# A two-layer relational graph convolution: 46 of 196 octets of layer 2 read h from SBUF instead of gathering rows, and GpSimd clears a few bytes behind each gather

## The chip, the cores and the metric

The kernel runs on one core of one Trainium2 chip. The metric is device time in microseconds (us), the median of several runs. A core has five engines with queues of their own: TensorE (PE, with its weight loads shown as PEld), VectorE (DVE), ScalarE (ACT), GpSimd (POOL) and SyncE (SP). They run side by side and wait for one another through semaphores. Sixteen DMA engines move data between HBM and the on-chip memory SBUF; matrix products land in PSUM, eight banks.

## The reference

There are 12500 nodes with 128 float32 features, and 200000 edges with a source, a target and one of 8 relations. The edges are sorted by target. Two layers are computed, then a residual and a layer norm:

```
for l in range(2):
    W     = einsum('rb,bio->rio', comp[l], basis[l])      # 8 relation weights, 128 x 128
    msgs  = (h @ W[r] for all r)[src, et]                 # one row per edge
    mean  = segment_sum(msgs, dst * 8 + et) / max(count, 1)
    h     = relu(mean.sum over relations + h @ root[l] + bias[l]) + h
out = layernorm(x + h)
```

## The kernel before

**Tiles.** The edges are cut into 1563 tiles of 128, one edge per partition, and eight tiles make an octet; there are 196 octets (NQ). The nodes are cut into 98 blocks of 128 (NT). h is held transposed, features on partitions: `hT`, the first 98 x 128 columns of a large SBUF tile named `arena`. Before h is written there, the same space holds the edge lists and scratch of the preparation.

**Preparation.** From the sorted targets the kernel works out, for each edge, its relation and target slot (`kr`), one over the count of its segment (`w`), its target relative to a window of the output (`near`) and the row that it reads: `idx`, the source in layer 1, and `idy`, source x 8 + relation, in layer 2. A series of guards (`fails`, `check_all`) makes sure that the sorted, windowed path holds for this input; otherwise a slow general path runs instead.

**Layer 1** (`for o in range(NG - 3)`). For each octet GpSimd gathers 8 times 128 rows of x from HBM with an indirect DMA (`gather`, line 678), five octets ahead (AHEAD) into a ring of seven buffers (`rows_r`). VectorE builds, per tile, a one-hot matrix times `w` (`onehot`, line 1122). TensorE multiplies rows by one-hot (`means`, L1215), ScalarE copies the sums out of PSUM (`take_means`, `copy` at L628), TensorE applies the eight relation weights (`product`, L1247), and `place` (L1278) adds the result to the block of 128 targets it belongs to. When a block is complete, `finish` adds bias, relu and residual on VectorE and writes `hT`. From octet 50 (TABLE) on, `table` (L1346) multiplies each finished block by all eight weights of layer 2, and the result (8 rows per node) is stored to HBM as `y_d`. One or two of these table halves go into each octet, in the banks `pt_b` and `ct_b`.

**Layer 2** (`for q in range(NQ)`). Since the weights are already applied, an edge only needs its row of `y_d`: GpSimd gathers it (the same line 678, by `idy`). VectorE builds small one-hots of 32 columns per tile and one of 256 per octet (`slot_hots`, L1091 and L1094). TensorE sums the rows by slot (`slot_sums`, L1442, eight 128 x 32 matmuls in the bank `misc`), ScalarE copies the 128 x 128 sums (`ys`), and one octet later TensorE places them in the block (`place_sums`, L1467, with the root weight L1471 when a block opens). Finished blocks are turned back and normalised, eight at a time (`norm`, L1585 to L1613). The last four octets (from FULL on) take another way (`add_rows`). After each octet up to there, `keep_on` issues 12 (BURST) float16 matmuls 128 x 384 whose result nobody uses (L1483).

**Order.** Everything is issued by a planner (`Plan`): the Python code calls `vec`, `act`, `pe`, `pool` and `load` in the order in which each engine's queue shall run, with the cells that an operation reads and writes, and the planner puts semaphore waits before those that need them. Engines signal only at marked places (`plan.mark`). A gather waits for the buffer that it fills to be read, seven octets back, and for the octet four back on its DMA semaphore to have landed (`lanes`: "gq" has 4):

```
t, cell = rows_r.take()
...
plan.add("POOL", some(i0, i0 + n), reads,
         [cell + (0,), cell + (1,)] + (fix_rows_c if fixes else []), lane="gq",
         n=n + fixes, after=after)
```

Once layer 1 is over, its tiles are used again: `home(where, n, ...)` hands out parts of old tiles to layer 2's buffers.

## Time and profile before

| | us |
|---|---|
| median of 3 runs | 4645.08 |
| lowest and highest | 4639.48, 4657.33 |
| profiled execution, its own time | 4616.74 |
| its span, first to last instruction | 4614.8 |
| layer 1's gathers, 1563, busy | 1476.4 |
| layer 2's gathers, 1563, busy | 1475.0 |

Busy shares of the whole span: TensorE 53%, its weight loads 37%, VectorE 30%, ScalarE 10%, GpSimd 64%. The mean granted clock of TensorE is 0.723 of its full speed. The DMA engines moved 284.99 MB, 62 GB/s.

How to read the rows: a group names the line of the kernel, the engine, the operation, output<-input by the names of the tiles, and a count; then busy time in us and the mean of one in ns; then the idle time of the engine just before these instructions and what ended most of it. "issue" is idle time in which the engine waited for nothing that the profile shows; "remote" is a wait whose releaser the profile did not find. A timeline row has the start in us from the beginning, the length, the engine and the operation, and in brackets the idle time before it. Matmuls overlap in the pipeline, so the sum of their lengths is more than their busy time.

### The profile page before, as it was taken

How to read it: one execution, taken by the hardware profiler on the slowest of the kernel's cores; microseconds unless marked ns; L12 is line 12 of the kernel's file. 1: busy time of each engine (PE TensorE's matmuls, PEld its weight loads, DVE VectorE, ACT ScalarE, POOL GpSimd, SP SyncE). 2: the span in 40 equal slices, each digit the busy share in tenths (PEclk: the TensorE clock that was granted, in tenths of full speed). 3: DMA queues.
4: the chain of work that ended last, by engine and by line, in shares of the span. 5: the costliest groups of instructions: out<-in, count | busy, mean ns of one | idle time of the engine just before them, and what ended most of it. 6: DMA issues, size and time to landing. Idle time of an engine off the chain costs nothing.

```text
span 4614.8 us, 38428 instructions
## 1 busy us (share of the span) xinstructions
PE 2424.3 (53%) x14055; PEld 1713.5 (37%) x14055; DVE 1386.0 (30%) x4891; ACT 465.8 (10%) x1141; POOL 2953.5 (64%) x3135
## 2 busy tenths in 40 slices
PE   2666666555666566666644444444444444444445
PEld 1555554444555455555521222222222222222223
DVE  2544333333333233233312222222222222222223
ACT  0111112121211111111200000000000000000000
POOL 5666666666666666666556666666666666666664
PEclk9878777878777777777866666666666666666667
DMA  3111122223222222222221111112211212122121
GB/s 100 45 50 46 45 63 86 86 90 93 86 69 73 73 70 73 63 74 68 74 74 45 46 55 47 55 46 56 56 46 55 55 47 56 46 55 55 47 55 45
DMA packets 129830, 284.99 MB, mean 62 GB/s; under 512 B 54019, under 2 KB 61773, under 8 KB 129637
## 3 DMA queue, kind: packets, MB, share of 16 engines
q0 software_dynamic: 100064, 205.13, 17.1%
q10 hardware_dynamic: 16971, 52.05, 2.9%
q1 hardware_dynamic: 12602, 25.31, 1.6%
q8 instruction: 112, 1.84, 0.2%
q14 instruction: 81, 0.66, 0.0%
HBM read 223.63 MB, written 58.65 MB: 61 GB/s over the span
## 4 chain that ended last, share of the span: by engine, by line
another core or an unknown queue 41%; PE 32%; issue 20%; ACT 5%; DVE 2%; POOL 0%; DMA 0%; SPq 0%; ACTq 0%; POOLq 0%; DVEq 0%
PE y L1247 8%; PE y L1483 7%; PE s L1215 5%; PE po L1442 3%; ACT sT L628 2%; PE s L1467 2%; PE pt L1346 2%; PE po L1278 1%; ACT ys L628 1%; ACT y_row L628 1%; PE ct L1346 1%; DVE dm L1122 1%; PE po L1280 0%; PE s L1471 0%
## 5 line engine op out<-in xcount | busy, mean ns | idle before, releaser
L678 POOL DMA_INDIRECT rows<-in_x_dram,idx x1563 | 1476.4, 945 | 841.5 <-issue 438.7
L678 POOL DMA_INDIRECT rows<-y_d,idy x1563 | 1475.0, 944 | 768.9 <-issue 447.6
L1247 PE MATMUL y<-w_sb,sT 128*128 128x128 f32 x3136 | 544.9, 345 | 533.3 <-ACT ys L628 236.4
L1483 PE MATMUL y<-id_h 128*128 128x384 f16 x2304 | 598.3, 398 | 342.9 <-issue 335.2
L1247 PEld LDWEIGHTS y<-w_sb,sT 128*128 128x128 f32 x3136 | 512.0, 255 | 558.1 <-ACT ys L628 245.2
L1122 DVE TENSOR_SCALAR dm<-cols,kr,w 128x128 f32<-128x128 f16 x1563 | 526.1, 402 | 493.4 <-remote 232.4
L1091 DVE TENSOR_SCALAR sT<-cols,kr,w 128x32 f32<-128x32 f16 x1536 | 352.8, 302 | 724.7 <-remote 543.4
L1442 PE MATMUL po<-rows,sT 128*32 128x128 f32 x3072 | 173.5, 354 | 712.1 <-ACT ys L628 437.4
L1215 PEld LDWEIGHTS s<-dm,rows 128*128 128x128 f32 x3126 | 434.5, 217 | 175.3 <-ACT sT L628 106.3
L1483 PEld LDWEIGHTS y<-id_h 128*128 128x128 f16 x2304 | 259.7, 114 | 643.2 <-issue 563.8
L1215 PE MATMUL s<-dm,rows 128*128 128x128 f32 x3126 | 451.2, 303 | 81.3 <-ACT sT L628 61.7
L1442 PEld LDWEIGHTS po<-rows,sT 128*32 128x32 f32 x3072 | 102.2, 136 | 799.8 <-ACT ys L628 463.5
L628 ACT ACTIVATE sT<-s 128x512 f32<-128x512 f32 x391 | 212.4, 596 | 804.5 <-remote 543.6
L628 ACT ACTIVATE ys<-po 128x128 f32<-128x128 f32 x192 | 53.2, 277 | 2111.9 <-remote 1871.6
L1299 DVE TENSOR_TENSOR po<-po,carry 128x128 f32<-128x128 f32 x98 | 29.2, 298 | 663.1 <-remote 406.8
L1299 DVE TENSOR_TENSOR s<-s,carry 128x128 f32<-128x128 f32 x97 | 28.9, 298 | 616.4 <-remote 387.7
L1346 PE MATMUL pt<-w_sb,arena 128*128 128x512 f32 x258 | 156.3, 678 | 48.5 <-issue 41.2
L1467 PE MATMUL s<-pl,ys 128*128 128x256 f32 x288 | 139.6, 572 | 14.3 <-issue 14.2
L1278 PE MATMUL po<-pl,ys 128*128 128x256 f32 x392 | 138.9, 438 | 15.1 <-DVE pl L1130 6.5
L628 ACT ACTIVATE y_row<-pt 128x512 f32<-128x512 f32 x131 | 78.4, 598 | 659.2 <-remote 451.3
L1585 PE MATMUL po<-ident,wide 128*128 128x128 f32 x96 | 23.5, 388 | 193.6 <-ACT ys L628 153.3
L871 PE MATMUL ct<-arena,id_h 128*128 128x512 f16 (+1 forms) x188 | 75.5, 422 | 85.9 <-issue 44.5
(214 smaller groups left out, 1565.0 us busy)
## 6 DMA issues: line engine op xcount, KB each, us to landing
y_d<-y_row ACTq DMA_DIRECT2D x96, 512.0 KB
rows<-in_x_dram,idx POOLq DMA_INDIRECT x1563
rows<-y_d,idy POOLq DMA_INDIRECT x1563
x_g<-in_x_dram SPq DMA_DIRECT2D x24, 512.0 KB
out_dram<-x_g SPq DMA_DIRECT2D x12, 512.0 KB
arena<-in_L_gnn_basis_dram SPq DMA_DIRECT2D x2, 512.0 KB
w_d<-y_row SPq DMA_DIRECT2D x2, 512.0 KB
w_sb<-w_d SPq DMA_DIRECT2D x2, 512.0 KB
```

The source lines that it names most:

```text
L628: act(lambda: nc.scalar.activation(out_t, in_t, AF.Copy), reads, writes)
L678: ins.append(nc.gpsimd.indirect_dma_start(out=t[:, i - q * Q, :], out_offset=None, in_=table_t, in_offset=bass.IndirectOffsetOnAxis(ap=ids ...
L871: nc.tensor.matmul(ct[:, :nb, :], id_h, eq[:, s - s0, :nb, main], start=(s == 1), stop=False)
L1091: vec(in_turn([lambda i=i: nc.vector.tensor_scalar(t[:, i, :], cols[:, :2 * K], kr[:, i0 + i:i0 + i + 1], w[:, i0 + i:i0 + i + 1], op0=ALU ...
L1122: emits.append(lambda i=i: nc.vector.tensor_scalar(t[:, i - q * Q, :wide], cols[:, :wide], ids[:, i:i + 1], w[:, i:i + 1], op0=ALU.is_equa ...
L1215: last = nc.tensor.matmul(s_b[i // 4][0][:, i % 4, :], t[:, i, :], d[:, i, :], start=True, stop=True)
L1247: last = nc.tensor.matmul(y[:m], t[:, r, :nt, :].rearrange("p t k -> p (t k)"), w_sb[:, 0, r, :], start=(r == 0), stop=(r == R - 1))
L1278: ins = nc.tensor.matmul(a, o[:m], t[:m], start=opens, stop=last and not root_in)
L1346: pe(lambda: nc.tensor.matmul(hb[:n].rearrange("p r d -> p (r d)"), hT[:, j * P:j * P + n], w_sb[:, 1, k * H:(k + 1) * H, :].rearrange("p ...
L1442: last = nc.tensor.matmul(m0[i // 2 * 2 * K:(i // 2 + 1) * 2 * K, :], d[:, i, :], t[:, i, :], start=i % 2 == 0, stop=i % 2 == 1)
L1467: ins = nc.tensor.matmul(a, o[:m], t[:m], start=opens, stop=last and not root_in and not fixed)
L1483: last = nc.tensor.matmul(f[:, :3, :], id_h, rhs, start=True, stop=True)
```

## The change

Four things change.

1. **Routed octets.** Every fourth octet of layer 2 from 8 to 188, 46 in all (`ROUTED`), is no longer gathered. Its rows are picked on the chip from h. For that, `hT` is turned, block by block and in place, into rows (nodes on partitions) after the tables of a block are made: `turn_rows`, four blocks at a time, as further entries of the `tables` list in layer 1, and `turn_last` for the last six at the start of layer 2. `open_block` then turns a block back where layer 2 needs it transposed.
2. **Sorting in layer 1.** In layer 1, octets 96 to 142, the edges of one routed octet at a time are sorted into slots, for each half octet (BR = 2) 49 groups of 256 source nodes with 32 slots each (CAP): `groups_of` and `ranks_of` on VectorE, `earlier_of` and `slots_of` on TensorE, two ScalarE copies and three stores to HBM (`lo_d`, `sc_d`) on SP. `values` prepares the numbers for all 46 among the checks.
3. **Routing in layer 2.** The 46 x 7 steps (`route_step`) are spread over the octets, seven per four octets. A step compares the slots' node numbers with the partition number (`compare`, VectorE, two operations of 512 columns), picks rows of h by these one-hots (`pick_rows`, TensorE, 32 matmuls 128 x 32, and a ScalarE copy), makes one-hots of target and relation times the weight (`slots_in`, VectorE, four of 320 columns) and adds up (`add_up`, TensorE, four matmuls 320 wide). Once per octet the sums go through the eight relation weights (`relate`), and the result enters `place_sums` as a gathered octet's does. `slot_sums` moves to the bank `ct_b`. `keep_on` is removed.
4. **Clearing.** After every gather GpSimd clears 256 bytes per partition of a scratch tile in layer 1 and 128 in layer 2 (`pause`), and each clearing waits for the one before it.

Two guards are added to `fails`, one for the window of 40 target nodes and one for the 32 slots. The core of the diff:

```diff
-    BURST = 12
     DONE = NT - 4
     FULL = NQ - 4
+    BT = 4
+    CAP = 32
+    NW = 40
+    GU = P // CAP
+    NGH = -(-NT // 2)
+    NTL = -(-NGH // GU)
+    NGR = NTL * GU
+    TU = 4
+    SEG = R * NW
+    BR = 2
+    WHOLE = [[(b, v, GU) for v in range(u, u + TU)] for b in range(BR) for u in range(0, NTL - 1, TU)]
+    REST = [(b, NTL - 1, NGH - (NTL - 1) * GU) for b in range(BR)]
+    STEPS = WHOLE[:len(WHOLE) // 2] + [REST] + WHOLE[len(WHOLE) // 2:]
+    NU = len(STEPS)
+    EVERY = 4
+    TURN = 4
+    LATER = NT - 6
+    FROM = 1
+    ROUTED = list(range(FROM + 10 * EVERY // NU + 2, 192, EVERY))
+    NR = len(ROUTED)
+    SORT = 96
...
+    blank = keep([P, P // 2], F32, "blank").bitcast(mybir.dt.uint8)
+    paused, pauses = tc.alloc_semaphore("s_pause"), [0]
+
+    def pause(n):
+        if pauses[0]:
+            nc.gpsimd.wait_ge(paused, pauses[0])
+        nc.gpsimd.memset(blank[:, :n], 0).then_inc(paused, 1)
+        pauses[0] += 1
...
-        if q >= NQ:
+        if q >= NQ or l == 1 and q in ROUTED:
...
+                    pause((2 * P, P)[l])
...
+    def groups_of(j):
+        o, oc = oh_b[j % 2]
+        o3 = o.bitcast(F16).rearrange("p (t g) -> p t g", t=Q)
+        vec(lambda: nc.vector.tensor_tensor(
+            o3, cols[:, None, :NGR].to_broadcast([P, Q, NGR]), grp[:, j, :].unsqueeze(2).to_broadcast([P, Q, NGR]),
+            op=ALU.is_equal), ["cols", grp_b[1]], [oc])
+
+    def earlier_of(j):
+
+        o, oc = oh_b[j % 2]
+        o4 = o.bitcast(F16).rearrange("p (b t g) -> p b t g", b=2, t=BT)
+        b, bc = ct_b
+        c4 = b.rearrange("p t d -> p (t d)")[:, :Q * NGR].rearrange("p (b t g) -> p b t g", b=2, t=BT)
+
+        def emit():
+            last = nc.tensor.matmul(c4, tri, o4, start=True, stop=False)
+            for k in range(1, BT):
+                last = nc.tensor.matmul(c4[:, :, k:, :], every, o4[:, :, :BT - k, :], start=False, stop=k == BT - 1)
+            return last
+
+        pe(emit, [oc, tri_b[1], one_b[1]], [bc])
...
+    def ranks_of(j):
+        (o, oc), (vv, vc), (jt, jc), (ct, cc) = oh_b[j % 2], v_b[j % 2], j_b, count_b
+        b, bc = ct_b
+        o3 = o.bitcast(F16).rearrange("p (t g) -> p t g", t=Q)
+        c3 = ct.rearrange("p (t g) -> p t g", t=Q)
+        b3 = b.rearrange("p t d -> p (t d)")[:, :Q * NGR].rearrange("p (t g) -> p t g", t=Q)
+        j3 = jt.bitcast(F16).rearrange("p (t c) -> p t c", t=Q)
+        v4 = vv.bitcast(F16).rearrange("p (t v c) -> p t v c", t=Q, v=3)
+        vec(lambda: nc.vector.tensor_tensor(c3, b3, o3, op=ALU.mult), [bc, oc], [cc])
+        vec(lambda: nc.vector.tensor_reduce(rank[:, j, :], c3, axis=AX.X, op=ALU.add), [cc], [rank_b[1] + (j,)])
+        vec(lambda: nc.vector.tensor_tensor(
+            j3, cols[:, None, :CAP].to_broadcast([P, Q, CAP]), rank[:, j, :].unsqueeze(2).to_broadcast([P, Q, CAP]),
+            op=ALU.is_equal), ["cols", rank_b[1] + (j,)], [jc])
+        vec(lambda: nc.vector.tensor_tensor(
+            v4, j3[:, :, None, :].to_broadcast([P, Q, 3, CAP]), val[:, j].unsqueeze(3).to_broadcast([P, Q, 3, CAP]),
+            op=ALU.mult), [jc, val_b[1]], [vc])
...
+    def turn_rows(j0, b, bc):
+
+        j1 = min(j0 + TURN, NT)
+
+        def first_step():
+            def emit():
+                for j in range(j0, j1):
+                    n = rows_of(j)
+                    last = nc.tensor.transpose(b[:n, j - j0, :], hT[:, j * P:j * P + n], ident)
+                return last
+
+            pe(emit, [("h", j) for j in range(j0, j1)] + ["ident"], [bc])
+
+        def second_step(copy=copy):
+            parts = [(j0, j1)] if rows_of(j1 - 1) == P else [(j0, j1 - 1), (j1 - 1, j1)]
+            for a, c in parts:
+                n = rows_of(a)
+                copy(hT[:n, a * P:c * P].rearrange("p (j d) -> p j d", d=P), b[:n, a - j0:c - j0, :], [bc],
+                     [("h", j) for j in range(a, c)])
+            turned_back.update(range(j0, j1))
+
+        return first_step, second_step
...
+    def compare(t):
+
+        i, u = t // NU, t % NU
+        if i >= NR:
+            return
+        at_u = STEPS[u]
+        b0, v0, m = at_u[0]
+        (o, oc), (b, bc) = hot_b[t % 3], bits_b[i % 2]
+        b3 = b.bitcast(F16).rearrange("p (b n) -> p b n", b=BR)
+        if m == GU:
+            n, a = HC, b3[:, b0, v0 * P:v0 * P + HC]
+            outs = [o[:, c * HC:c * HC + n] for c in range(2)]
+        else:
+            n, a = m * CAP, b3[:, :, v0 * P:v0 * P + m * CAP]
+            outs = [o[:, c * HC:c * HC + BR * n].rearrange("p (b n) -> p b n", b=BR) for c in range(2)]
+        vec(in_turn([lambda c=c: nc.vector.tensor_scalar(outs[c], a, node_p[:, c:c + 1], None, op0=ALU.is_equal)
+                     for c in range(2)]), [bc, "node"], new(oc))
+        plan.mark("DVE")
...
+    def slots_in(t):
+
+        i, u = t // NU, t % NU
+        sg, sgc = segw_b[i % 2]
+        for b, v, m in STEPS[u]:
+            o, oc = slot_at(i, b, v)
+            n, x = m * CAP, b * NTL + v
+            vec(lambda o=o, n=n, x=x: nc.vector.tensor_scalar(
+                o[:n], segs[:n], sg[:n, x:x + 1], sg[:n, BR * NTL + x:BR * NTL + x + 1], op0=ALU.is_equal,
+                op1=ALU.mult), [segs_b[1], sgc], new(oc))
+        plan.mark("DVE")
...
+    def pick_rows(t):
+        i, u = t // NU, t % NU
+        (o, oc), (g, gc) = hot_b[t % 3], rows_b[t % 3]
+        b, bc = pt_b
+        at_u = STEPS[u]
+
+        def emit():
+            for x, (_, v, m) in enumerate(at_u):
+                for k in range(m):
+                    at = (x * m + k) * CAP
+                    for c in range(2):
+                        j = 2 * (v * GU + k) + c
+                        n = rows_of(j)
+                        last = nc.tensor.matmul(b[k * CAP:(k + 1) * CAP, x, :], o[:n, c * HC + at:c * HC + at + CAP],
+                                                hT[:n, j * P:(j + 1) * P], start=c == 0, stop=c == 1)
+            return last
+
+        js = sorted({2 * (v * GU + k) + c for _, v, m in at_u for k in range(m) for c in range(2)})
+        pe(emit, [oc] + [("h", j) for j in js], [bc])
+        plan.mark("PE")
+        n, m = len(at_u), at_u[0][2] * CAP
+        copy(g[:m, :n * P], b[:m, :n, :].rearrange("p t d -> p (t d)"), [bc], new(gc))
+        plan.mark("ACT")
...
+    def add_up(t):
+        i, u = t // NU, t % NU
+        g, gc = rows_b[t % 3]
+        at_u = STEPS[u]
+
+        def emit():
+            for x, (b, v, m) in enumerate(at_u):
+                o, n = slot_at(i, b, v)[0], m * CAP
+                z = order[b, v]
+                last = nc.tensor.matmul(seg_b[b][0].rearrange("p t d -> p (t d)")[:, :SEG], g[:n, x * P:(x + 1) * P],
+                                        o[:n], start=z in (0, NTL), stop=z in (NTL - 1, BR * NTL - 1))
+            return last
+
+        bs = sorted({b for b, _, _ in at_u})
+        pe(emit, [gc] + [slot_at(i, b, v)[1] for b, v, _ in at_u], [seg_b[b][1] for b in bs])
+        plan.mark("PE")
+        for k in range(BR):
+            if u == (NU // 2, NU - 1)[k]:
+                t_s, sc = sum_b[i % 2]
+                t4 = t_s.rearrange("p (r b n) -> p r b n", r=R, b=BR)
+                b, bc = seg_b[k]
+                copy(t4[:, :, k, :], b.rearrange("p t d -> p (t d)")[:, :SEG].rearrange("p (r n) -> p r n", r=R), [bc],
+                     new(sc + (k,)))
+                plan.mark("ACT")
...
+    def relate(i):
+        t_s, sc = sum_b[i % 2]
+        t4 = t_s.rearrange("p (r b n) -> p r b n", r=R, b=BR)
+        b, bc = misc
+        pe(in_turn([lambda r=r: nc.tensor.matmul(
+            b[:BR * NW, 0, :], t4[:, r].rearrange("p b n -> p (b n)"), w_sb[:, 1, r, :], start=r == 0, stop=r == R - 1)
+            for r in range(R)]), [sc + (k,) for k in range(BR)] + [("w", 1, r) for r in range(R)], [bc])
+        plan.mark("PE")
+        o, c = ys[ROUTED[i]] = ys_r.take()
+        copy(o[:BR * NW], b[:BR * NW, 0, :], [bc], [c])
+        plan.mark("ACT")
...
+    def route_step(t):
+
+        i, u = t // NU, t % NU
+        if u == 0 and i < NR:
+            unit_rows(i)
+        compare(t + 1)
+        if i < NR:
+            pick_rows(t)
+        if 0 <= t - 1 < NR * NU:
+            slots_in(t - 1)
+        if 0 <= t - 2 < NR * NU:
+            add_up(t - 2)
+        if u == 3 and i >= 1 and i - 1 < NR:
+            relate(i - 1)
+        if u == 1:
+            fetch_rows(i + 1)
+        if u == NU - 1:
+            fetch(i + 2)
...
-    def keep_on():
-        f = y_full[0]
-        rhs = id_h[:, None, :].to_broadcast([P, 3, P])
-
-        def emit():
-            for _ in range(BURST):
-                last = nc.tensor.matmul(f[:, :3, :], id_h, rhs, start=True, stop=True)
-            return last
-
-        pe(emit, ["id_h"], [y_full[1]])
...
+        if 0 <= o - SORT - 1 < NR:
+            ranks_of(o - SORT - 1)
+        if 0 <= o - SORT < NR:
+            groups_of(o - SORT)
+        plan.mark("DVE")
...
+                if i == 1 and SORT - 2 <= o < SORT + NR + 2:
+                    break
...
+        if q == 0:
+            turn_last()
+        if q == FROM - 1:
+            compare(0)
+        route(q, 0)
...
+        route(q, 1)
...
-            keep_on()
...
```

239 lines of the change are left out of this document (226 added, 13 removed).

## The prediction

> **What bounds the kernel now.** I read the page first, then the waits of GpSimd, then a table by stage, then the timeline of single engines. The page's span and its two groups of gathers (line, engine, operation, count, busy us, mean ns, idle before):
>
> ```profile
> span 4614.8 us, 38428 instructions
> ...
> L678 POOL DMA_INDIRECT rows<-in_x_dram,idx x1563 | 1476.4, 945 | 841.5 <-issue 438.7
> L678 POOL DMA_INDIRECT rows<-y_d,idy x1563 | 1475.0, 944 | 768.9 <-issue 447.6
> ```
>
> GpSimd's waits (us in total, times, longest):
>
> ```profile
> POOL rows L678 <- remote: 550.5, 200, 9.5
> POOL rows L678 <- PE s L1215: 118.1, 19, 30.9
> ```
>
> Three stages (from and to, length; busy us and count of PE, PEld, DVE, ACT, POOL; granted clock, DMA share, GB/s), the first in layer 1:
>
> ```profile
> 110.00:1200.00 1090.00, 683.63 (x3865) 566.85 (x3864) 416.19 (x1253) 184.15 (x396) 703.73 (x745) 0.79 0.24 69
> ...
> 2400.00:3000.00 600.00, 246.39 (x1542) 123.58 (x1546) 140.64 (x577) 20.70 (x78) 394.08 (x418) 0.64 0.18 50
> ...
> 3600.00:4560.00 960.00, 422.05 (x2730) 221.68 (x2731) 256.18 (x1053) 33.98 (x137) 624.90 (x662) 0.66 0.19 51
> ```
>
> GpSimd's gathers pace both layers. A gather is 0.944 us busy; with 0.30 us of issue it would recur every 1.25 us. But layer 1 takes 1090/745 = 1.46 us per gather, layer 2 takes 1560/1080 = 1.44. The rest, some 0.2 us, are the waits "remote" and "PE". The DMA engines are idle four fifths of the time, so no bandwidth holds them. What does is seen in the timeline, first VectorE's and GpSimd's at the start (start, length, engine, line):
>
> ```profile
> 48.06 0.67 DVE L861 TENSOR_TENSOR arena<-cols,arena 128x149 f16<-128x149 f16 x4 [18.97 <-remote]
> 70.46 0.67 DVE L861 TENSOR_TENSOR arena<-cols,arena 128x153 f16<-128x153 f16 x4 [21.73 <-remote]
> ...
> 86.27 0.70 DVE L861 TENSOR_TENSOR arena<-cols,arena 128x165 f16<-128x165 f16 x4 [0.34 <-PE ct L872]
> ```
>
> ```profile
> 75.32 0.94 POOL L678 DMA_INDIRECT rows<-in_x_dram,idx  x1 [0.30 <-issue]
> 107.16 0.94 POOL L678 DMA_INDIRECT rows<-in_x_dram,idx  x1 [30.90 <-PE s L1215]
> ```
>
> A ping-pong of VectorE and TensorE needs some 20 us a round while GpSimd gathers back to back (until 75.32), and under 1 us once it stands still (86.27). So gathers 1.25 us apart hold up the other engines' handovers. The same in layer 2, TensorE, ScalarE and GpSimd:
>
> ```profile
> 3472.67 0.67 PE L1442 MATMUL po<-rows,sT 128*32 128x128 f32 x16
> 3473.26 0.70 PE L1467 MATMUL s<-pl,ys 128*128 128x256 f32 x2
> 3473.80 2.11 PE L1483 MATMUL y<-id_h 128*128 128x384 f16 x12
> 3488.43 1.10 PE L1442 MATMUL po<-rows,sT 128*32 128x128 f32 x16 [12.52 <-issue]
> 3489.47 1.22 PE L1467 MATMUL s<-pl,ys 128*128 128x256 f32 x2
> 3490.48 0.64 PE L1471 MATMUL s<-id_r,w_sb 128*128 128x128 f32 x2
> ...
> 3497.24 0.48 PE L1483 MATMUL y<-id_h 128*128 128x384 f16 x1 [2.46 <-issue]
> ```
>
> ```profile
> 3488.10 0.28 ACT L628 ACTIVATE ys<-po 128x128 f32<-128x128 f32 x1 [18.85 <-remote]
> ```
>
> ```profile
> 3492.08 0.94 POOL L678 DMA_INDIRECT rows<-y_d,idy  x1 [0.30 <-issue]
> 3493.33 0.94 POOL L678 DMA_INDIRECT rows<-y_d,idy  x1 [0.31 <-issue]
> ...
> 3519.92 0.94 POOL L678 DMA_INDIRECT rows<-y_d,idy  x1 [0.30 <-issue]
> 3524.07 0.94 POOL L678 DMA_INDIRECT rows<-y_d,idy  x1 [3.21 <-remote]
> ```
>
> ScalarE copies at 3488.10 the sums that were multiplied at 3472.67. GpSimd meanwhile fills its seven row buffers and then stands 3.2 us (3519.92 to 3524.07). Sixteen gathers and one such stall are 16 x 1.25 + 2.9 = 22.9 us, 1.43 each. That every stage comes out near 1.4 suggests a limit there, from which a pitch of 1.25 only borrows.
>
> **The change, part by part.** The reckoning is against the profiled execution, 4616.7 us (its span 4614.8 and 1.9 around it); the median of the three runs shown, 4645.1, lies 28 us above it, which is added at the end.
>
> *Fewer gathers.* 46 x 8 = 368 gathers of layer 2 go: at 1.44 us that is 530 us of GpSimd, the most the routing can give. The unit to compare is a period of four octets, one of them routed: now 32 x 1.44 = 46.1 us.
>
> *The clearing.* Behind each gather stands a memset that waits for the memset before it, done over 1 us earlier; behind it queues the next gather. The nearest rows are GpSimd's first instructions:
>
> ```profile
> 1.52 0.12 POOL L764 IOTA part<- 128x1 int32 x1
> 1.60 0.34 POOL L765 IOTA iota_f<- 128x256 f32 x1
> 1.91 0.34 POOL L767 IOTA arena<- 128x224 int32 x1
> ```
>
> From start to start, one element takes 0.08 us and 256 take 0.31, by line 128 take 0.19. A fill of bytes may be quicker than an iota of words, so the lower end is 0.08 for both sizes; the upper is an iota's pitch plus another issue gap of 0.30, 0.5 and 0.6. I take 0.17 for 128 bytes and 0.22 for 256, near the iotas. What covers it: the waits of 550.5 + 118.1 us, 0.21 per gather, which the spacing must make needless. If they stay, it costs 1563 x 0.22 + 1195 x 0.17 = 550 us in full. Layer 1 then is 1.25 + 0.22 = 1.47 per gather against 1.46: nothing, with ends of -0.08 x 1563 = -125 (a short fill) and +0.35 x 1563 = +550 (a long one). The stand of 30.90 us at the start should shrink: I take -20.
>
> *Layer 1's new work.*
>
> ```profile
> L1593 DVE TENSOR_TENSOR x_g<-po,x_g 128x512 f32<-128x512 f32 x24 | 16.6, 692 | 241.5 <-PE po L1585 157.4 <-remote 84.2
> ```
>
> In octets 96 to 142 VectorE gets a one-hot of 416 elements and four operations of 256 to 768, by this row 3 us an octet: it is busy 416.19/1090 = 38%, 4.5 us of 11.7, and becomes 7.5. TensorE gets 12 short f16 matmuls an octet and 98 transposes in all, some 30 us; ScalarE 25 copies of 0.6 and two small ones an octet; SP three small stores an octet, ahead of x loads that nobody waits for. From octet 94 to 143 the tables lose their second place an octet and catch up after. All are hidden behind 11.7 us of gathers; without that cover the routing's part is 46 x 3 = 140 us. The last turns, the rank check and the first fetches at the border of the layers come where GpSimd waits for the table anyhow: +5.
>
> *TensorE in layer 2.* The 12 filler matmuls an octet go and the picks come. From start to start, eight matmuls 128x32 (3472.67) take 0.59 us in the quick stretch and 1.04 in the slow one (3488.43); a placing 256 wide 0.54 and 1.01. Picking is 24 such groups of eight and a small rest; 0.59 holds a drain and a wait, so back to back I take 0.45 (0.32 to 0.59): 11.2. Adding up is 26 matmuls 320 wide, at most 0.54 x 320/256 = 0.68 each, taken 0.58: 15.1. The eight relation weights 2; four placings 2.2; three slot sums 1.8; roots, transposes and norm 1.5. Sum 34 us a period; 38 by the upper ends; 61 at the slow stretch's prices. GpSimd needs 24 x 1.42 = 34.
>
> *VectorE in layer 2.* Today 256.18 us for 662/8 octets, 3.1 an octet. A routed one needs 12 compares of 512 elements (at most 0.69, taken 0.5) and 26 slots of 320 (0.27, the pitch in the row below, to 0.69; taken 0.45): 18, and 1.5 for the rest. A period: 3 x 3.1 + 19.5 = 29, at most 38. ScalarE needs 7. SP fetches 0.85 MB per routed octet, one octet ahead; with the DMA engines 19% busy this is covered.
>
> Here a rule speaks against the change. The row:
>
> ```profile
> 3492.26 2.16 DVE L1613 TENSOR_SCALAR x_g<-x_g,st 128x128 f32<-128x128 f32 x8
> ```
>
> These are eight operations from SBUF to SBUF as the new ones are, and the gathers at 3492.08 and 3493.33 beside them keep their 0.94 us and 1.25 us pitch. The Trainium skill, SBUF — State Buffer, section "SBUF: two separate sides", says that such VectorE operations can lock GpSimd out of a shared port for their whole length and so starve its descriptors. By that rule the 18 us of new work would come on top of GpSimd's 34. The trace does not agree with it here; it stays as rival C.
>
> *Sum.* GpSimd 34, TensorE 34, VectorE 29 a period: three engines so close, coupled by handovers, won't overlap fully, nor is the clock full throughout. I add 15% to 34: 39.5. Layer 2: 46 x (46.1 - 39.5) = -304. Start, border and layer 1: -15. 4616.7 - 304 - 15 = 4298; with the 28, 4326, say 4330.
>
> **The rivals.**
> *A, the forecast:* a period of 37 to 42, 4210 to 4445. For it: 34 us of work against 46 of gathers, and the routing leaves a whole step (some 5 us) between each maker and user.
> *B, slower: TensorE becomes the bound,* at a low clock or with handovers still held up. Layer 2's granted clock is 0.64 to 0.66, and at 3497.24 a matmul that waits for nothing is issued 2.46 us late. 34 us at a clock of 0.68 are 50 us: 46 x 4 = +184, 4815. It decides above 46 us a period. Against it: where work is dense (3472.67) the prices are the low ones. The Trainium skill, TensorE: Matmul & The Clock Gate, Part 1, says that the clock halves after some 3.4 us of idling and is whole after as long a busy time; by that B needs waits, not work.
> *C, the port:* 34 us of GpSimd and 18 of VectorE in turn, 52: 46 x 6 = +276, 4905. It needs gathers that grow beside VectorE, which the rows deny.
> *D, GpSimd alone still paces:* both fills fit under 1.40, TensorE keeps up: a period of 34, -557, and layer 1 -95 to -125: 3950 to 4100.
> *E, a long fill:* 256 bytes cost 0.35, layer 1 +0.13 x 1563 = +203, layer 2 as in A: 4530.
> That the guards send the kernel to its general path is as good as excluded: in the reference's own inputs a half octet spans at most 37 nodes of 40 and fills 22 slots of 32.
>
> **How the numbers follow.** Chances: A 0.52, D 0.17, E 0.11, B 0.16, C 0.04. Within 0.5%, about what a measurement can tell, lies only the edge between E and B: 0.04. Faster takes A, D and most of E, 0.78; slower B and C with the worst of E, less that edge, 0.18. The range leaves out most of D, B and C below and above: 4080 to 4690.
>
> **What will show it.** Right: layer 2 has 1195 gathers; GpSimd's stalls of 3 us become even gaps; 24 gathers take near 39.5 us; TensorE's granted clock in layer 2 rises above 0.8; waits like 18.85 (ScalarE) shrink to a few us; 30.90 is shorter. Wrong: a pitch in layer 1 outside 1.40 to 1.55; gathers longer than 0.944 beside VectorE's compares; TensorE busy throughout at a low clock.

## The result, and the profile after

The changed kernel takes 5170.66 us, median of 4 runs (5162.00 to 5175.56); the kernel before, on the same chip, 4649.89 (4639.48 to 4657.33). The ratio is 1.112, with a 95% interval of 1.1091 to 1.1148: 11% slower, where 7% faster was forecast. Chips differ here, so a ratio is always taken against the kernel before on the same chip, and the text says how long that one took there.

The page of the kernel after, span and the two groups of gathers; below it, GpSimd's waits and the longest ones of ScalarE and VectorE:

```profile
span 5160.1 us, 81490 instructions
...
L741 POOL DMA_INDIRECT rows<-y_d,idy x1195 | 1162.6, 973 | 1321.4 <-PE ct L1882 1129.9
L741 POOL DMA_INDIRECT rows<-in_x_dram,idx x1563 | 1502.7, 961 | 301.7 <-issue 259.0
```

```profile
ACT sT L683 <- remote: 1274.4, 164, 53.1
POOL rows L741 <- PE ct L1882: 1129.9, 131, 56.1
DVE arena L1743 <- remote: 564.1, 75, 8.2
```

Layer 2 has 1195 gathers instead of 1563, but GpSimd now stands 1129.9 us before them, waiting for TensorE (L1882 is `slot_sums`, which reads the row buffers). The stages, with the columns as before (length; busy us and count of PE, PEld, DVE, ACT, POOL; clock, DMA share, GB/s):

```profile
110.00:1200.00 1090.00, 684.42 (x3918) 577.77 (x3917) 435.51 (x1312) 184.84 (x395) 950.30 (x1486) 0.81 0.23 66
2400.00:3000.00 600.00, 441.91 (x5106) 309.11 (x5110) 240.78 (x788) 60.91 (x150) 337.66 (x550) 0.86 0.17 48
3600.00:4560.00 960.00, 748.87 (x8667) 526.13 (x8666) 415.19 (x1372) 99.66 (x252) 493.43 (x800) 0.88 0.17 49
```

POOL counts two instructions per gather now, the gather and its memset. Layer 1 does 1486/2 = 743 gathers in the stretch where the kernel before did 745: unchanged. Layer 2 does 800/2 = 400 in 960 us, 2.40 us each; a period of four octets has 24, so 57.6 us against 46.1 before. No engine is full: TensorE 78%, GpSimd 51%, VectorE 43%, ScalarE 10%. It is 2814 us from the first to the last gather of layer 2, 2268 before: these 546 us are the whole loss, for the spans differ by 5160.1 - 4614.8 = 545.3.

The pitch inside a run of gathers (timeline of GpSimd near the start, in layer 1, then in layer 2):

```profile
74.71 0.95 POOL L741 DMA_INDIRECT rows<-in_x_dram,idx  x1 [0.17 <-issue]
...
110.75 0.95 POOL L741 DMA_INDIRECT rows<-in_x_dram,idx  x1 [0.17 <-issue]
...
600.65 0.95 POOL L741 DMA_INDIRECT rows<-in_x_dram,idx  x1 [0.17 <-issue]
601.59 0.34 POOL L703 MEMSET blank<- 128x256 uint8 x1
602.09 0.95 POOL L741 DMA_INDIRECT rows<-in_x_dram,idx  x1 [0.17 <-issue]
...
2320.86 0.95 POOL L741 DMA_INDIRECT rows<-y_d,idy  x1 [3.38 <-DMA y_d<-y_row]
...
2322.19 0.95 POOL L741 DMA_INDIRECT rows<-y_d,idy  x1 [0.17 <-issue]
2323.14 0.22 POOL L703 MEMSET blank<- 128x128 uint8 x1
2323.53 0.95 POOL L741 DMA_INDIRECT rows<-y_d,idy  x1 [0.16 <-issue]
```

With 256 bytes it is 602.09 - 600.65 = 1.44 us, with 128 bytes 1.34 (the median over layer 2 is 1.335). Without clearing it was 1.25. So 256 bytes cost 0.19 us and 128 only 0.085: the memset takes 0.22 us, but the issue gap in front of the next gather shrinks from 0.30 to 0.17. What happens between the runs of gathers (timeline of PE, ACT and POOL):

```profile
3502.71 0.28 ACT L683 ACTIVATE ys<-ct 128x128 f32<-128x128 f32 x1
...
3506.51 1.22 PE L1774 MATMUL pt<-arena,dm 128*32 128x128 f32 x8 [0.23 <-issue]
...
3512.66 0.95 POOL L741 DMA_INDIRECT rows<-y_d,idy  x1 [0.17 <-issue]
3513.19 0.60 ACT L683 ACTIVATE idx<-pt 128x512 f32<-128x512 f32 x1 [10.20 <-remote]
3513.84 3.48 PE L1774 MATMUL pt<-arena,dm 128*32 128x128 f32 x64 [4.58 <-issue]
...
3524.75 0.66 PE L1882 MATMUL ct<-rows,sT 128*32 128x128 f32 x16
...
3525.51 0.28 ACT L683 ACTIVATE ys<-ct 128x128 f32<-128x128 f32 x1 [2.40 <-PE ct L1882]
3525.74 0.95 POOL L741 DMA_INDIRECT rows<-y_d,idy  x1 [11.91 <-PE ct L1882]
```

By the rows, TensorE has picked the rows of h at 3507.73 (3506.51 + 1.22); ScalarE copies them 5.5 us later, at 3513.19, in the middle of the last gather of the run. TensorE, which has stood for 4.58 us by then, goes on at 3513.84, when the gather has just ended. Now GpSimd stands 11.91 us, until TensorE has worked itself forward to `slot_sums` (3524.75), which frees the row buffers. Then the next eight gathers follow, and the others stand again. GpSimd and the rest of the core take turns instead of working side by side.

### The profile page after: what moved, and what is told of

Read it like the earlier page. It is cut to its first block, busy times and chain, and to the rows that moved or that the text cites. A ratio compares the mean times of both kernels' runs of the same rounds, so it can differ in the third digit from the quotient of the medians.

```text
span 5160.1 us, 81490 instructions
## 1 busy us (share of the span) xinstructions
PE 3621.2 (70%) x32975; PEld 2733.0 (53%) x32975; DVE 2162.5 (42%) x6759; ACT 712.4 (14%) x1673; POOL 3482.7 (67%) x5525
## 4 chain that ended last, share of the span: by engine, by line
PE 51%; another core or an unknown queue 27%; issue 13%; ACT 4%; DVE 3%; POOL 2%; DMA 0%; ACTq 0%; POOLq 0%; DVEq 0%
PE pt L1774 12%; PE y L1318 8%; PE y L1796 7%; PE po L1796 6%; PE s L1286 5%; ACT sT L683 2%; PE po L1820 2%; PE pt L1417 2%; PE po L1349 2%; PE ct L1882 1%; POOL rows L741 1%; PE s L1907 1%; PE ct L1417 1%; DVE dm L1193 1%
## 5 line engine op out<-in xcount | busy, mean ns | idle before, releaser
L741 POOL DMA_INDIRECT rows<-y_d,idy x1195 | 1162.6, 973 | 1321.4 <-PE ct L1882 1129.9
L1774 PE MATMUL pt<-arena,dm 128*32 128x128 f32 (+1 forms) x18032 | 959.5, 313 | 463.1 <-ACT sT L683 208.5
L1774 PEld LDWEIGHTS pt<-arena,dm 128*32 128x32 f32 (+1 forms) x18032 | 723.3, 123 | 668.4 <-issue 283.4
L703 POOL MEMSET blank<- 128x256 uint8 (+1 forms) x2758 | 821.7, 298 | 1.6
L1743 DVE TENSOR_SCALAR arena<-y_row,sel 128x320 f32<-128x320 f16 (+1 forms) x598 | 235.0, 447 | 578.9 <-remote 299.2
L1743 DVE TENSOR_SCALAR arena<-y_row,comp_sb 128x320 f32<-128x320 f16 (+1 forms) x598 | 234.9, 448 | 572.8 <-PE y L1796 288.6
L1796 PE MATMUL po<-arena,sT 128*128 128x320 f32 (+1 forms) x798 | 275.3, 480 | 16.2 <-issue 15.3
L1724 DVE TENSOR_SCALAR dm<-arena,pair 128x512 f32<-128x512 f16 (+1 forms) x644 | 263.3, 458 | 9.5 <-remote 6.1
L1796 PE MATMUL y<-arena,sT 128*128 128x320 f32 x798 | 257.6, 458 | 3.6 <-issue 1.9
L1796 PEld LDWEIGHTS po<-arena,sT 128*128 128x128 f32 (+1 forms) x798 | 156.9, 207 | 110.9 <-issue 68.5
```

What stands on the lines that cost most here:

```text
L703: nc.gpsimd.memset(blank[:, :n], 0).then_inc(paused, 1)
L741: ins.append(nc.gpsimd.indirect_dma_start(out=t[:, i - q * Q, :], out_offset=None, in_=table_t, in_offset=bass.IndirectOffsetOnAxis(ap=ids ...
L1724: vec(in_turn([lambda c=c: nc.vector.tensor_scalar(outs[c], a, node_p[:, c:c + 1], None, op0=ALU.is_equal) for c in range(2)]), [bc, "node ...
L1743: vec(lambda o=o, n=n, x=x: nc.vector.tensor_scalar(o[:n], segs[:n], sg[:n, x:x + 1], sg[:n, BR * NTL + x:BR * NTL + x + 1], op0=ALU.is_equal,
L1774: last = nc.tensor.matmul(b[k * CAP:(k + 1) * CAP, x, :], o[:n, c * HC + at:c * HC + at + CAP], hT[:n, j * P:(j + 1) * P], start=c == 0, s ...
L1796: last = nc.tensor.matmul(seg_b[b][0].rearrange("p t d -> p (t d)")[:, :SEG], g[:n, x * P:(x + 1) * P], o[:n], start=z in (0, NTL), stop=z ...
```

## The experiments

Three theories stood against each other. The spacing theory: gathers that follow one another too closely hold up the handovers between the other engines, and 1.33 us is too close. The work theory: the routing itself costs TensorE, VectorE or a shared port this much. The per-gather theory: each gather holds the others up by a fixed amount, however it is spaced.

The chips turned out to be of two kinds. On some the kernel before takes 4613 to 4653 us, on one 3928. The one of 3928 was met a single time, so what sets it apart is not known, nor whether it lasts. The table gives the results; pitch is the median from gather to gather in layer 2, layer 2 runs from its first gather to its last, and the period is that length over 49.

| run | layer 2 clears | kernel before, us | this, us | ratio, 95% interval | pitch | layer 2, us | period |
|---|---|---|---|---|---|---|---|
| e3 | nothing | 3928 | 3714.41 | 0.9457, 0.9441 to 0.9472 | 1.25 | 1730 | 35.3 |
| e1 | 256 B | 3928 | 4136.57 | 1.0533, 1.0516 to 1.0551 | 1.44 | 1838 | 37.5 |
| e5, routing alone | 128 B | 3928 | 4011.19 | 1.0212, 1.0192 to 1.0233 | | 1717 | 35.0 |
| e4, clearing alone | 128 B | 3928 | 4385.65 | 1.1166, 1.1147 to 1.1184 | 1.33 | 2101 | |
| e8 | nothing | 4617 | 5264.92 | 1.1411, 1.1389 to 1.1434 | 1.25 | 2894 | 59.1 |
| e6 | 128 B | 4614 | 5054.34 | 1.0951, 1.0932 to 1.0969 | 1.34 | 2739 | 55.9 |
| e7 | 128 B | 4617 | 5059.22 | 1.0957, 1.0934 to 1.0981 | 1.34 | 2752 | 56.2 |
| e9 | 256 B | 4617 | 4777.69 | 1.0352, 1.0333 to 1.0370 | 1.44 | 2474 | 50.5 |
| e16 | 320 B | 4653 | 4706.94 | 1.0125, 1.0097 to 1.0153 | 1.50 | 2359 | 48.1 |
| e17 | 320 B | 4650.5 | 4716.75 | 1.0145, 1.0125 to 1.0164 | 1.50 | 2367 | 48.3 |
| e18 | 384 B | 4650.5 | 4443.63 | 0.9554, 0.9527 to 0.9581 | 1.55 | 2099 | 42.8 |
| e15 | 384 B | 4614 | 4274.16 | 0.9267, 0.9249 to 0.9285 | 1.55 | 1976 | 40.3 |
| e11 | 512 B | 4613 | 4358.34 | 0.9443, 0.9422 to 0.9465 | 1.66 | 2056 | 42.0 |
| e12 | 768 B | 4613 | 4555.09 | 0.9871, 0.9851 to 0.9892 | 1.87 | 2249 | 45.9 |
| e14 | 4 x 832 B per octet | 4614 | 5142.45 | 1.1137, 1.1109 to 1.1165 | 1.25 | 2851 | 58.2 |
| e13, routing alone | 128 B | 4613 | 4046.71 | 0.8769, 0.8744 to 0.8793 | | 1739 | 35.5 |
| e10, clearing alone | 128 B | 4617 | 4545.78 | 0.9844, 0.9826 to 0.9861 | 1.34 | 2254 | |

### The parts one by one, where the kernel before takes 3928 us

**e1: 256 bytes in layer 2 too.**

```diff
-                    pause((2 * P, P)[l])
+                    pause(2 * P)
```

> The changed kernel, but 256 bytes cleared behind layer 2's gathers too. Theory H (gathers closer than about 1.40 us hold up the other engines' handovers; 1.334 us in layer 2 of the changed kernel is too close): the pitch becomes 1.44, the waits of 8 to 12 us in layer 2 go, a period of four octets falls from 57 to about 40 us, the time to 4300 to 4500. Theory W (the routing's own work and chain of handovers need 57 us a period whatever GpSimd does): the period stays at 55 to 58, the time at 5100 to 5200.

**e3: the routing without the clearing.**

```diff
-                    pause((2 * P, P)[l])
```

> The changed kernel without any clearing: gathers 1.25 us apart. H: layer 2 gets worse than the changed kernel's 57 us a period, 60 or more, and the stalls of 3 us are back in layer 1, whose length stays within 1%; 5250 or more. W: layer 2 as in the changed kernel, 5150 to 5200.

**e4: the clearing without the routing**, put into the kernel before.

```diff
                         in_offset=bass.IndirectOffsetOnAxis(ap=ids[:, i:i + 1], axis=0)))
+                    pause((2 * P, P)[l])
```

> The kernel before with the clearing alone (256 and 128 bytes), no routing, the filler matmuls kept. H: the clearing fills the time that stalls took, 4600 to 4700 in all. If instead the clearing adds to the stalls: 1563 x 0.19 + 1563 x 0.085 = +430, about 5080.

**e5: the routing with hardly a gather beside it**, one of eight in layer 2.

```diff
-            plan.add("POOL", some(i0, i0 + n), reads,
+            m = 1 if l == 1 and SOON // Q < q < NQ - 4 else n
+            plan.add("POOL", some(i0, i0 + m), reads,
```

> The changed kernel with one gather of eight in the octets 3 to 191 of layer 2 (seven of eight tiles sum rows that are old, so the result is not the reference's): TensorE, VectorE and ScalarE keep all their work. H: the period is TensorE's own work, 37 to 42 us, the time 4250 to 4450. W: 55 us or more, 5000 to 5200.

All four fell on a chip on which nothing is held up, and none of the four times lies where it was expected: the kernel before takes 3928 us there, and in e4, which has all its gathers, GpSimd has next to no stand. The groups of gathers on the page of e4, and layer 2's in e3:

```profile
L686 POOL DMA_INDIRECT rows<-in_x_dram,idx x1563 | 1487.9, 952 | 271.2 <-issue 265.9
L686 POOL DMA_INDIRECT rows<-y_d,idy x1563 | 1487.4, 952 | 269.1 <-issue 269.1
```

```profile
L741 POOL DMA_INDIRECT rows<-y_d,idy x1195 | 1268.8, 1062 | 461.2 <-issue 349.8
```

In e4 nearly all idle time is "issue", the 0.17 us before each instruction. There the clearing is a plain cost, 1563 x (0.19 + 0.085) = 430 us worked out and 4385.65 - 3928.07 = 458 measured, and the routing alone, e3, gains 5.4%. Layer 2 of e3 and of e5 (a stretch of 600 us each):

```profile
2700.00:3300.00 600.00, 595.06 (x8845) 443.74 (x8844) 421.57 (x1411) 106.92 (x258) 441.36 (x410) 1.00 0.27 79
```

```profile
2700.00:3300.00 600.00, 595.06 (x8891) 444.45 (x8894) 421.03 (x1418) 106.78 (x258) 67.62 (x102) 1.00 0.13 41
```

TensorE is busy 99% at a clock of 1.00 in both, with 410 gathers in the stretch or with some 50; the period is 35.3 and 35.0 us. So the routing's own work is 35 us of TensorE a period, nothing is lost to gathers beside it, and the work theory cannot account for 57. What this chip could not show is the holding up itself.

### The change again, and its parts, where the kernel before takes 4614 us

**e6 and e7: the changed kernel, unedited**, beside the kernel before.

> The changed kernel itself, beside the kernel before, where the kernel before gathers without stalls (3928 us, 1.257 us per gather). Theory S (the clearing is pure cost wherever the handovers aren't held up; the routing saves): layer 1 grows by 1563 x 0.19 = 300, layer 2 is TensorE's 36 us a period plus what the memsets add, together 4030 to 4110, 2 to 5% slower than the 3928. Theory F (the two kernels stand as in the recorded pair): 1.11 times the kernel before, 4370.

> The changed kernel once more, so that the three kernels beside it can be held against it on the same chip. Where the kernel before needs some 4600 us: 1.10 times that, as twice before. Where it needs some 3930: by the parts, layer 1 + 300 and layer 2 near TensorE's 36 us a period, 4030 to 4110.

**e8: e3's kernel. e9: e1's. e10: e4's.**

> The changed kernel without any clearing. Where the kernel before needs some 3930 us: again 3714. Where it needs some 4600 us: theory H says that gathers 1.25 us apart hold up handovers, that the routing has many more of them than the kernel before and so loses more than with the clearing: 5100 or more. Theory K (the clearing costs there as well, and the routing alone pays): below the kernel before, 4300 to 4500.

> The changed kernel with 256 bytes cleared in layer 2 too, 1.44 us per gather. Where the kernel before needs some 3930 us: again 4137. Where it needs some 4600 us: theory H says that 1.44 is wide enough, layer 2's period falls from 57 to 40 us, 4300 to 4500; if the handovers stay held up, above 4900.

> The kernel before with the clearing alone, no routing. Where the kernel before needs some 3930 us: again 4386. Where it needs some 4600 us: theory H says that the clearing takes the place of the stalls, 4500 to 4650; if it adds to them, 5000.

The loss is there again, 9.5%. Taking the clearing out makes it worse (e8, 1.141), more of it makes it better (e9, 1.035), though e9's 4778 us lie between its two expectations, 4300 to 4500 and above 4900. GpSimd's stands for TensorE in layer 2, in e8 and in e9:

```profile
POOL rows L741 <- PE ct L1881: 1347.0, 135, 56.1
```

```profile
POOL rows L741 <- PE ct L1882: 646.7, 87, 50.7
```

The clock of e9 rises with it, against 0.86 to 0.88 in the kernel after:

```profile
2700.00:3300.00 600.00, 513.90 (x6181) 365.67 (x6182) 312.06 (x991) 74.53 (x180) 385.07 (x567) 0.93 0.19 55
```

The kernel of e8 stands 103.4 us for this wait in e3, on the other chip:

```profile
POOL rows L741 <- PE ct L1881: 103.4, 21, 45.0
```

Routing, code and data are the same, and layer 2 takes 1730 us on the one chip and 2894 on the other. And e10 separates the parts from the other side: without the routing the clearing costs nothing on this chip but gains 1.6%, its 0.19 and 0.085 us a gather taking the place of stands, just as the prediction had it.

### More room behind each gather

**e11: 512 bytes in layer 2. e12: 768 bytes.** The scratch tile is too small for it, so `base`, free by then, is cleared.

```diff
-        nc.gpsimd.memset(blank[:, :n], 0).then_inc(paused, 1)
+        t = blank if n <= 2 * P else base.rearrange("p b a c -> p (b a c)").bitcast(mybir.dt.uint8)
+        nc.gpsimd.memset(t[:, :n], 0).then_inc(paused, 1)
...
-                    pause((2 * P, P)[l])
+                    pause((2 * P, 4 * P)[l])
```

> The changed kernel with 512 bytes cleared behind layer 2's gathers (by 0.107 us per 128 bytes a pitch of 1.66 us, 24 gathers 40 us). Where the kernel before needs some 4600 us: theory H, that only the spacing of the gathers is short, says the handovers come free, a period of 40 to 43 us, 4270 to 4420, faster than the kernel before; if every gather holds them up whatever the spacing (theory G), the time stays near the 4778 of 256 bytes or above. Where it needs some 3930: GpSimd paces layer 2, 2280 + 1990 = 4280.

> The same with 768 bytes, a pitch of 1.87 us, 24 gathers 45 us. H: GpSimd paces layer 2 evenly, 45 to 46 us a period, 4500 to 4560 on either kind of chip. G: above 4700 where the kernel before needs some 4600.

**e13: e5's kernel**, nearly without gathers.

> The changed kernel with one gather of eight in the octets 3 to 191 of layer 2 (seven of eight tiles sum old rows). H and G: with the gathers nearly gone nothing holds up the handovers, layer 2 runs at TensorE's own 35 us a period also where the kernel before needs some 4600 us: 4010 to 4060. If that chip has slow handovers for another reason than gathers: 4500 or more.

The stands are gone: in e11 all of GpSimd's idle time before layer 2's gathers but 2.5 us is issue. With its gathers a quarter further apart (1.66 for 1.34) the change takes 14% less time (0.9443 against 1.0951). The page of e11, and layer 2 of e11 and of e13:

```profile
L742 POOL DMA_INDIRECT rows<-y_d,idy x1195 | 1156.3, 968 | 196.4 <-issue 193.9
```

```profile
2700.00:3300.00 600.00, 546.65 (x7655) 404.31 (x7646) 472.18 (x1236) 91.73 (x222) 542.84 (x696) 0.97 0.23 66
```

```profile
2700.00:3300.00 600.00, 595.05 (x8830) 445.25 (x8829) 415.24 (x1397) 106.13 (x257) 68.53 (x100) 1.00 0.12 39
```

e13 has the same 595 us of 600 and the same clock as on the chip of 3928 us. That refutes the work theory for this chip as well, and e11 refutes the per-gather theory: it has all 1195 gathers, and no copy is held up for long (counted below). With 768 bytes GpSimd is full, and something else shows, which the last section takes up.

### The gap or the mean rate

**e14: the same mean rate as e11, but in bursts.** The eight gathers of an octet follow one another without clearing, and four memsets of 832 bytes stand behind them.

```diff
-                    pause((2 * P, P)[l])
+                    if l == 0:
+                        pause(2 * P)
+                for _ in range(4 * (l == 1 and i1 - i0 == Q)):
+                    pause(6 * P + 64)
```

> The changed kernel, with layer 2's clearing behind each gather taken out and four clearings of 832 bytes put behind every eight gathers instead. Gathers of an octet then follow one another at about 1.25 us, and the mean pitch stays near 1.65. If the mean rate decides (the chip's kernel before near 4615): no handover is held up, layer 2 as with 512 bytes, some 2060 us, the whole about 4360. If the gap behind each gather decides: TensorE and ScalarE stand for most of each burst of 8 x 1.25 = 10 us and catch up in the pause of about 3 us; an octet then takes 13 to 16 us, layer 2 2150 to 2500, the whole 4450 to 4800. On a chip whose kernel before takes near 3930 nothing is held up in either case, and GpSimd paces at about 1.65: layer 1 2290, layer 2 2030 to 2060, the whole about 4350.

**e15: 384 bytes**, e11's edit with `3 * P`.

> The changed kernel with 384 bytes cleared behind each gather of layer 2: a pitch of about 1.55, between 1.44 (256 bytes) and 1.66 (512). If handovers come free at a point below 1.55: GpSimd paces, 1.55 x 1195 and a little more, layer 2 1900 to 1950 us, the whole 4200 to 4260, faster than with 512 bytes. If they come free step by step: layer 2 between the 2474 and 2056 us of its neighbours, about 2200 to 2350, the whole 4500 to 4650. On a chip whose kernel before takes near 3930: GpSimd paces, the whole about 4200 to 4240.

e14 takes 5142 us, longer even than with 128 bytes (5054), though its eight gathers and four memsets could recur every 8 x 1.25 + 3.42 = 13.4 us, the 8 x 1.66 = 13.3 of e11. It was expected at up to 4800 for this theory; the holding up costs more than I had reckoned. The timeline of e14, POOL, PE and ACT:

```profile
3503.36 0.95 POOL L742 DMA_INDIRECT rows<-y_d,idy  x1 [0.31 <-issue]
...
3510.87 0.95 POOL L742 DMA_INDIRECT rows<-y_d,idy  x1 [0.30 <-issue]
3511.81 3.42 POOL L704 MEMSET base<- 128x832 uint8 x4
...
3520.81 1.09 POOL L742 DMA_INDIRECT rows<-y_d,idy  x1 [5.58 <-PE ct L1886]
```

```profile
3506.32 0.50 PE L1778 MATMUL pt<-arena,dm 128*32 128x128 f32 x3 [0.26 <-issue]
...
3514.22 1.11 PE L1778 MATMUL pt<-arena,dm 128*32 128x128 f32 x16 [4.14 <-ACT idx L683]
```

```profile
3513.57 0.60 ACT L683 ACTIVATE idx<-pt 128x512 f32<-128x512 f32 x1 [11.43 <-remote]
```

The picked rows are complete at 3506.82 and are copied at 3513.57, 1.8 us after the last gather of the burst, though GpSimd goes on clearing. Two later bursts end the same way: their last gathers end at 3545.83 and 3564.57, and ScalarE, after waits of 9.73 and 11.43 us, copies at 3547.53 and 3566.32. So it is the gathers and not GpSimd's being busy, and what counts is the room behind each single one, not the rate at which GpSimd could gather on average. In e15, with 384 bytes behind each gather, ScalarE's copies in the same stretch of time have short waits, and layer 2 is busy:

```profile
3505.40 0.60 ACT L683 ACTIVATE sT<-pt 128x512 f32<-128x512 f32 x1 [2.76 <-PE pt L1775]
3508.36 0.28 ACT L683 ACTIVATE ys<-ct 128x128 f32<-128x128 f32 x1 [2.36 <-PE ct L1883]
...
3529.01 0.60 ACT L683 ACTIVATE idx<-pt 128x512 f32<-128x512 f32 x1 [4.18 <-remote]
```

```profile
2700.00:3300.00 600.00, 572.32 (x7871) 417.35 (x7871) 454.03 (x1255) 93.87 (x229) 538.82 (x732) 1.00 0.24 71
```

It takes 4274 us, ratio 0.9267: the shortest of the whole kernels run on chips of this kind. It was expected at 4200 to 4260 if the point lay below 1.55.

### How sharp the point is

**e16 and e17: 320 bytes**, e11's edit with `2 * P + 64`. **e18: e15's kernel once more.** They ran where the kernel before takes 4650 to 4653 us.

> The changed kernel with 320 bytes cleared behind each gather of layer 2: a pitch of about 1.50. On a chip whose kernel before takes near 4615: if the handovers come free at a point below 1.50, layer 2 is paced by GpSimd and TensorE together at some 38 to 39 us a period, 1880 to 1920 us, the whole 4180 to 4220, shorter than the 4274 with 384 bytes. If they come free step by step, layer 2 lies between the 2474 us of 256 bytes and the 1976 of 384, near 2225, the whole near 4520. On a chip whose kernel before takes near 3930: GpSimd paces, the whole about 4170 to 4210.

> The kernel with 320 bytes once more, beside the one with 384 on the same chip. If the pitch decides: again near 4.7 ms and over 300 us longer than with 384 bytes, with stalls of up to 50 us. If it was the chip: on a chip whose kernel before takes near 4615 it comes near 4200 and below the 384 bytes. On a chip whose kernel before takes near 3930 GpSimd paces, about 4190.

> The kernel with 384 bytes once more. If the pitch decides: near 4270 to 4300 on a chip whose kernel before takes 4615 or 4650. If it was the chip: near 4270 on the one of 4615, and 4600 or more on the one of 4650. On a chip whose kernel before takes near 3930 GpSimd paces, about 4220.

On one and the same chip 320 bytes give 4717 us and 384 bytes 4444. GpSimd's stands for TensorE in layer 2, e17 and then e18:

```profile
POOL rows L742 <- PE ct L1883: 471.7, 84, 51.2
```

```profile
POOL rows L742 <- PE ct L1883: 154.8, 36, 46.3
```

So pitch and chip both matter. 64 bytes more take two thirds of the stands away on this chip, and 155 us of them are left; on the chip of 4614 us, e15 stands once for 23.1 us and no more. Both expectations for e18 were too clean: it lies between them. And e16 lies above both of its own, 4180 to 4220 and near 4520.

GpSimd's stands are what comes of the holding up; the traces show it directly as well. For each of some 310 ScalarE copies of picked rows in layer 2 (`idx` or `sT` from `pt`), the table has how long the copy starts after the last pick has ended and ScalarE is free:

| layer 2 clears | run | copies over 3 us late | mean, us |
|---|---|---|---|
| nothing | e8 | 98 | 2.16 |
| 128 B | e6 | 121 | 2.29 |
| 256 B | e9 | 108 | 1.73 |
| 320 B | e16, e17 | 123, 118 | 1.92, 1.90 |
| 384 B | e18, e15 | 7, 0 | 1.40, 1.16 |
| 512 B | e11 | 0 | 0.55 |
| 768 B | e12 | 0 | 0.41 |
| 128 B, hardly a gather | e13 | 0 | 0.04 |
| nothing; 256 B, kernel before 3928 us | e3; e1 | 0; 0 | 0.06; 0.05 |

The long delays stay as many up to a pitch of 1.50 and are all but gone at 1.55; short ones remain and shrink as the spacing grows. So on these chips there is a fairly sharp point for the long delays, and no spacing tried is free of the short ones.

For the kernel as a whole 384 bytes beat the kernel before on the two chips of this kind on which they ran, and the change on the one where it ran too; where the kernel before takes 3928 us no clearing at all is best (e3).

## Why the prediction was wrong

**What bounds the kernel now.** The cause was named rightly: gathers 1.25 us apart hold up the other engines' handovers. The step that failed is the sentence that every stage comes out near 1.4, which "suggests a limit there, from which a pitch of 1.25 only borrows". I took the mean of 1.44 for a spacing at which handovers would be free, and so let GpSimd, TensorE and VectorE overlap at 34 us a period with 15% on top. It is no spacing; it is the sum of taking turns, runs at 1.25 and stands behind them, as the stall after sixteen gathers that I had worked out shows. How much there is to stand for depends on how many handovers lie between two runs. The routing adds to each octet steps that TensorE, ScalarE and VectorE hand to one another, and so a mean of 1.44 became one of 2814/1195 = 2.35, at a pitch that is wider than before. That it is the routing's steps is seen where the spacing is the same: at 1.34 us the mean is 2254/1563 = 1.44 without the routing (e10) and 2739/1195 = 2.29 with it (e6). At a real pitch of 1.44 the change still loses 3.5% (e9); it needed 1.55 (e15).

**The clearing.** For 128 bytes I took 0.17 us, between ends of 0.08 and 0.5; it measured 0.085, the lower end. For 256 bytes I took 0.22 and it measured 0.19. The difference matters in layer 2: 1.335 us from gather to gather where I had 1.42. By e6 and e9 the 128 bytes too few cost 5054 - 4778 = 276 us. That is the smaller part of the miss. From 1.44 to 1.55, the limit placed too low, it is 4778 - 4274 = 504. Three slips in the prediction's sums bear on no result: against 1.46 a fill of 0.08 is -0.13 a gather and one of 0.6 +0.39, not -0.08 and +0.35; TensorE's upper ends add up to 40, not 38; and 15% on 34 is 39.1, not 39.5.

**Fewer gathers.** 1195 remain, as said. The period of 46.1 us became 57.6, not 39.5. Once the spacing is wide enough the period comes near the 39.5: 40.3 in e15, and 4274 us for the whole, where 4330 was forecast. That it comes so near is partly luck: with the same 384 bytes it is 42.8 on another chip (e18), and the 15% stood for no particular wait.

**TensorE in layer 2.** 34 us a period were worked out from the quick rows, and 35.0 to 35.5 were measured with TensorE 99% busy (e5, e13). The prices of the slow stretch, 61 us, are of matmuls that follow a stand of 12.52 us (3488.43). The two prices of one row were no uncertainty of the work: they go with the two regimes, and which one the changed kernel would be in decided the result.

**VectorE and the port.** The compare took 0.482 us where I had 0.5, a slot operation 0.447 where I had 0.45 (rows in the last section). Rival C, 18 us a period on top, did not come: gathers are 973 ns in layer 2 against 961 in layer 1, 24 x 0.012 = 0.3 us a period. Even in e3, where they grow most, to 1062 ns, it is 24 x 0.109 = 2.6 us. The Trainium skill, SBUF — State Buffer, "SBUF: two separate sides", says that GpSimd cannot write descriptors while a VectorE operation in a two-port mode holds the shared port. The 18 us that C took from it did not come; the runs show 0.3 to 2.6.

**Layer 1, start and border.** Right in the main. Layer 1 does 743 gathers where it did 745, its new work is hidden, and the pitch of 1.44 lies in the 1.40 to 1.55 named. The stand of 30.90 us near the start is gone: from 74.71 to 110.75 us the kernel after gathers 25 times, one each 1.44 us. But the 15 us put down for start and border are not gained: layer 2's first gather starts at 2320.86 us, at 2322.4 before. Where the layers meet GpSimd stands 3.38 us (2320.86) and then 27.1 for the last table store, 26.5 before.

**The rivals.** D came nowhere: with no clearing and nothing held up TensorE paces, not GpSimd, and a period is 35.3 us, not 34 (e3); where GpSimd paces without stands its clearing is long, and the period is 42.0 (e11) and 45.9 (e12). E fell with the 0.19 us of 256 bytes. B came, in its second form, handovers still held up, with 57.6 us where its price was 50. It had a chance of 0.16, and what I set against it, that prices are low where work is dense, begs the question, since gathers in between decide whether work can be dense. Its clock is a symptom: 0.86 to 0.88 in layer 2 after, 0.93 in e9, and 1.00 in e13 and e15, at the same work. The Trainium skill, TensorE: Matmul & The Clock Gate, Part 1, has the clock follow idling, and these clocks agree. What I had not thought of as a rival is the chip: where the kernel before takes 3928 us there is no holding up at all, the clearing is a loss and the routing a gain.

## What to carry to other kernels

A mean pitch made of quick runs and stands is no safe spacing: before costing a change at such a mean, ask how many handovers the change adds between two runs, and whether the room really lies behind each single operation. Where one step has a quick and a slow price in the same trace, find out what separates them, and forecast which of the two the changed kernel will be in, instead of taking the quick one with a supplement. And measure a change of spacing on more than one chip: the same kernel won 5.4% on one and lost 14% on another.

## What the runs showed of the hardware

**Indirect gathers from GpSimd hold up handovers between other engines, on some chips and below some spacing.** With 1.25 us from gather to gather layer 2 of one and the same kernel took 1730 us on one chip and 2894 on another; with 1.55 us 1976 on the second, and 2099 on a third. That a copy waits for the end of the run of gathers is seen in e14 and in the kernel after. By what path a gather delays a signal or an instruction of another engine was not shown, whether by GpSimd's own work on it or by the transfers that it starts, nor why chips differ.

**A short memset in front of a gather costs less than its own length.** From the median pitches (1.25 with none, 1.335, 1.44, 1.50, 1.55, 1.66, 1.87) 128 bytes cost 0.085 us and each further 128 some 0.106, since the issue gap falls from 0.30 to 0.17.

**VectorE's operations take longer beside long memsets of GpSimd.** VectorE's compares and slot operations by shape, in the kernel after, with 768 bytes (e12), and nearly without gathers and memsets (e13):

```profile
L1724 DVE TENSOR_SCALAR dm<-arena,pair 128x512 f32<-128x512 f16 x552 | 243.0, 482 | 9.5 <-remote 6.1 <-DMA arena<-lo_d 3.3
L1743 DVE TENSOR_SCALAR arena<-y_row,comp_sb 128x320 f32<-128x320 f16 x552 | 215.5, 447 | 530.7 <-remote 264.9 <-PE y L1796 246.5 <-PE po L1796 15.5
```

```profile
L1744 DVE TENSOR_SCALAR arena<-y_row,comp_sb 128x320 f32<-128x320 f16 x552 | 473.7, 914 | 12.8 <-PE po L1797 7.2 <-PE y L1797 5.2
L1725 DVE TENSOR_SCALAR dm<-arena,pair 128x512 f32<-128x512 f16 x552 | 444.7, 844 | 3.4 <-DMA arena<-lo_d 3.4
```

```profile
L1725 DVE TENSOR_SCALAR dm<-arena,pair 128x512 f32<-128x512 f16 x552 | 236.6, 469 | 3.4 <-DMA arena<-lo_d 3.3
L1744 DVE TENSOR_SCALAR arena<-y_row,comp_sb 128x320 f32<-128x320 f16 x552 | 211.9, 442 | 174.1 <-PE y L1797 134.7 <-PE po L1797 39.2
```

With 768 bytes behind each gather the slot operations take twice as long, and VectorE is 94% busy in layer 2 (562.76 of 600 us):

```profile
2700.00:3300.00 600.00, 507.41 (x6868) 372.32 (x6867) 562.76 (x1103) 82.12 (x200) 547.24 (x639) 0.95 0.21 61
```

So clearing is no free way of waiting. The Trainium skill, SBUF — State Buffer, section "SBUF: two separate sides", says that VectorE and GpSimd share a pair of ports which one holds while the other stands; these rows agree with it for GpSimd's own memory operations, where of its gathers the runs show little. The slowing bears on e12, and on part of what 512 bytes lose against 384; it was not measured apart.
